# Row maxima of the larger query tiles: turned by a small product and placed by a 4 KB DMA, where the queries were transposed a second time

## The chip, the cores and the metric

The kernel runs on one core of a Trainium2 chip. The core has a matrix engine (TensorE, PE, with a separate path PEld for loading weights), a vector engine (VectorE, DVE), an activation engine (ScalarE, ACT), a general engine (GpSimd, POOL) and a sync engine (SyncE, SP), from whose queue nearly all transfers are issued. Each engine works through its own instructions in order; semaphores tie the engines together. On-chip memory is SBUF; matrix products land in PSUM, of which the kernel holds eight banks. The metric is the device time of one execution in microseconds.

## The reference

A macaron block over an input of 2 x 1024 tokens of width 1024: half a feed-forward layer, attention, half a feed-forward layer, each behind a layer norm and added to the residual. Cut to what matters:

```python
x = x + 0.5 * ffn(layernorm(x))      # gate, top 2 of 8, base weights, LoRA of rank 16 each
x = x + attention(layernorm(x))
x = x + 0.5 * ffn(layernorm(x))

# attention: 32 query heads, 8 key/value heads of 32 columns, causal
q, k = rope(h @ Wq), rope(h @ Wk)
att = q k^T / sqrt(32), masked above the diagonal
out = softmax(att) @ (h @ Wv) @ Wo
```

The softmax needs the maximum of each row of scores before the exponentials are taken. How this maximum comes to the place where it is subtracted is what the change is about.

## The kernel before, in words

The 2048 tokens are cut into 16 query tiles `t` of 128 tokens, eight to a batch element. Query tile `t` looks at `L = t % 8 + 1` key tiles (causal). Numbers are held as pairs of 16-bit halves, so that a product in 16 bits is as exact as one in 32 bits.

**Queries.** `q_out` (L556) writes the queries of a tile into `qst[t % 2]`, 128 tokens by 32 heads by 128 columns. Columns 0 to 95 of a head hold the query in three copies (high, high, low half), columns from 96 on are zero. `qt_load` (L626) takes the eight heads of two key/value heads (a pair `g - 1`, `g`) and transposes them through a DMA from SP's queue into a tile `qt` of 128 rows by 8 heads by 128 tokens, 256 KB. The keys, in `kts`, have three copies in rows 0 to 95 as well, rows 96 to 111 hold the constant -32768, the rest zero.

**First pass, `unit_s1` (L635).** For each key tile, four products `q^T k` give scores with the tokens in the partitions (L650, PE), into one of the three PSUM buffers `p_s1`, and VectorE reduces them to row maxima (L667). On the diagonal key tile, where `L > 2`, ScalarE copies the scores (L661), GpSimd masks them (L662) and VectorE reduces the copy. After the second head of a pair, L676 takes the maximum over the key tiles.

**The maximum into the queries.** The maximum, divided by 32768, is written as a high and a low half. Two ways exist:

- `L <= MPE` (3): the halves go into `mm`, 128 tokens by 16 columns at its end (L681, L682). `turned` remembers the pair. `turn_maxima` (L693) is called after the first score tile of the next unit, or by `unit_s2` if that comes first. It multiplies `mm` by an identity (L697), which turns the halves into rows 96 to 111 of a `p_s1` buffer, and VectorE spreads them over the eight heads in rows 96 to 111 of the `qt` tile that the first pass used (L699).
- `L > 3`: VectorE writes the halves into columns 96 and 97 of the eight heads in `qst` (L687, L688), and `qt_load` transposes these heads a second time into a new `qt` tile (L689).

Ten query tiles (`t % 8` from 3 to 7, twice) of four pairs each take the second way: 40 of the 104 transpositions issued at L630.

**Second pass, `unit_s2` (L799).** For each key tile one product `k^T q` over all 128 rows (L809, into `p_s2`) gives the scores with the keys in the partitions, and rows 96 on subtract the maximum. ScalarE takes the exponential (L815), which `av_batch` multiplies with the values (L745) and, after pairwise sums (`pair`, L723, DVE), with ones.

**Order.** `step(s)` runs one query tile: for each head the key tiles of `unit_s2`, with a piece of the first pass (`look`, `LOOK` = 6 to 3 heads ahead) and pieces of the dense layers (`stage_a1`, `stage_a2`, `stage_c1`, `stage_c2`; products at L409 to L411) between them. Streamed weights come through three buffers of 1 MB, `ws`, from SP's queue (L421). The normed rows are transposed by DMA (`tt`, L338) as are the keys (L553). A scheduler in the compiler layer then orders each engine's instructions by priority, by what waits for what, and by modelled durations. The `qt` pool has five buffers, `mm` is a single buffer.

Of the kernel before, what the change touches and what calls it, by code (L numbers as in the profile page):

```python
# [10 lines left out]
HP = mybir.dt.float16  # L11
I32 = mybir.dt.int32
AF = mybir.ActivationFunctionType
ALU = mybir.AluOpType
# [3 lines left out]
NH, NKV, DH, GRP = 32, 8, 32, 4  # L18
E, R = 8, 16
P = 128  # L20
KB = D // P
NT = B * T // P
TPB = T // P
EPS = 1e-5
XS = 1024.0
MROW = 32768.0
# [9 lines left out]
MPE = 3  # L36
# [8 lines left out]
def kernel(  # L45
# [16 lines left out]
    nc = tc.nc  # L62
# [5 lines left out]
    small = ctx.enter_context(tc.tile_pool(name="small", bufs=SB))  # L68
# [22 lines left out]
        out=cmask, in_=cmask, compare_op=ALU.is_ge, fill=-NEG, base=0,  # L91
# [6 lines left out]
        out=tri, in_=tri, compare_op=ALU.is_gt, fill=0.0, base=0,  # L98
# [9 lines left out]
    MR = 3 * DH  # L108
    MC = 2 * 2 * GRP
    ident16 = const.tile([P, P], HP)  # L110
# [3 lines left out]
    for i in range(2):  # L114
        nc.gpsimd.affine_select(
            out=picks, in_=picks, compare_op=ALU.not_equal, fill=1.0, base=-(MR + 2 * GRP * i),
# [12 lines left out]
    mms = stat.tile([P, MR + MC], HP, name="mm")  # L129
    nc.gpsimd.memset(mms, 0.0)  # L130

    xts, Ts = {}, {}
# [405 lines left out]
    KT, VA, QS, CTX, CT = {}, {}, {}, {}, {}  # L538
# [87 lines left out]
    def qt_load(t, g):  # L626

        assert ready[t] == 2 or g * GRP < NH // 2
        q = qtp.tile([P, 2 * GRP, P], HP, name="qt")
        nc.sync.dma_start_transpose(  # L630
            out=q, in_=QS[t][:, g * GRP : (g + 2) * GRP, :].rearrange("p h c -> p (h c)")
        )
        return q

    def unit_s1(t, g):  # L635

        b0 = t - t % TPB
        L = t - b0 + 1
        odd = g % 2
        if not odd:  # L640
            Ts["mx"] = small.tile([P, 2, TPB, GRP], FP, name="mx", bufs=2)
        mx = Ts["mx"]
        q = Ts["q1", (t, g - odd)][:, odd * GRP : (odd + 1) * GRP, :]
        for j in reversed(range(L)):
            ps = p_s1.tile([P, GRP, P], FP, name="s1")
            diag = j == L - 1
            off = diag and L > LOFF
            pem = diag and not off
            for h in range(GRP):
                nc.tensor.matmul(  # L650
                    ps[:, h, :], lhsT=q[0 : 3 * DH, h, :], rhs=KT[b0 + j][0 : 3 * DH, g, :],
                    start=(not pem or h == 0), stop=not pem,
                )
            if pem:
                nc.tensor.matmul(
                    ps, lhsT=negid, rhs=cmask.unsqueeze(1).to_broadcast([P, GRP, P]),
                    start=False, stop=True,
                )
            if off:
                sm = pp.tile([P, GRP, P], FP, name="sm", bufs=1)  # L660
                nc.scalar.copy(sm, ps)  # L661
                nc.gpsimd.affine_select(  # L662
                    out=sm, in_=sm, compare_op=ALU.is_ge, fill=-3.0e38, base=0,
                    pattern=[[0, GRP], [-1, P]], channel_multiplier=1,
                )
                ps = sm
            nc.vector.tensor_reduce(mx[:, odd, j, :], ps, AX.X, ALU.max)  # L667
            if turned:
                turn_maxima()
            yield  # L670
        if not odd:
            return
        q1 = Ts.pop(("q1", (t, g - 1)))
        if L > 1:
            m = small.tile([P, 2, GRP], FP, name="m4")
            nc.vector.tensor_reduce(m, mx[:, :, 0:L, :].rearrange("p a j h -> p a h j"), AX.X, ALU.max)  # L676
        else:
            m = mx[:, :, 0, :]
        if L <= MPE:
            mm = mms[:, MR:].rearrange("p (i a h) -> p i a h", i=2, a=2)  # L680
            nc.vector.tensor_scalar(mm[:, 0], m, 1.0 / MROW, None, ALU.mult)  # L681
            nc.vector.scalar_tensor_tensor(mm[:, 1], m, 1.0 / MROW, mm[:, 0], ALU.mult, ALU.subtract)  # L682
            turned.append((t, g - 1, q1))
            return
        qs = QS[t][:, (g - 1) * GRP : (g + 1) * GRP].rearrange("p (a h) c -> p a h c", a=2)
        mh, ml = qs[:, :, :, 3 * DH], qs[:, :, :, 3 * DH + 1]
        nc.vector.tensor_scalar(mh, m, 1.0 / MROW, None, ALU.mult)  # L687
        nc.vector.scalar_tensor_tensor(ml, m, 1.0 / MROW, mh, ALU.mult, ALU.subtract)  # L688
        Ts["q2", t, g - 1] = qt_load(t, g - 1)  # L689

    turned = deque()

    def turn_maxima():  # L693

        t, g, q1 = turned.popleft()
        ps = p_s1.tile([P, GRP, P], FP, name="s1")[:, 0, :]
        nc.tensor.matmul(ps[0 : MR + MC], lhsT=mms, rhs=ident16, start=True, stop=True)  # L697
        rows, heads = slice(MR, MR + MC), [MC, 2 * GRP, P]
        nc.vector.tensor_tensor(  # L699
            q1[rows], ps[rows].unsqueeze(1).to_broadcast(heads),  # L700
            picks[rows].unsqueeze(2).to_broadcast(heads), ALU.mult,
        )
        Ts["q2", t, g] = q1
# [95 lines left out]
    def unit_s2(t, g):  # L799
        b0 = t - t % TPB  # L800
        L = t - b0 + 1
        odd = g % 2
        while ("q2", t, g - odd) not in Ts:
            turn_maxima()
        q = (Ts.pop if odd else Ts.get)(("q2", t, g - odd))[:, odd * GRP : (odd + 1) * GRP, :]
        cs = S["cs", g // 4]
        for j in range(L):
            ps = p_s2.tile([P, GRP, P], FP, name="s2")
            ins = nc.tensor.matmul(  # L809
                ps.rearrange("p h k -> p (h k)"), lhsT=KT[b0 + j][:, g, :],  # L810
                rhs=q.rearrange("p h k -> p (h k)"), start=True, stop=True,
            )
            s2_ins.append(ins.ins)
            p32 = pp.tile([P, GRP, P], FP, name="p32", bufs=8)
            nc.scalar.activation(p32, ps, AF.Exp, scale=cs)  # L815
            if j == L - 1:
                nc.gpsimd.affine_select(  # L817
                    out=p32, in_=p32, compare_op=ALU.is_ge, fill=0.0, base=0,
                    pattern=[[0, GRP], [1, P]], channel_multiplier=-1,
                )  # L820
            av_add(t, g, j, L, p32)
            yield
# [46 lines left out]
    for h in range(2):  # L869
        for src, c in ((a_in, slice(0, P)), (g_in, slice(P, P + E))):  # L870
            pin(
                nc.sync.dma_start(
                    out=agst[:, h, :, c],
                    in_=src[h * (D // 2) : (h + 1) * (D // 2), :].rearrange("(k p) n -> p k n", p=P),
# [137 lines left out]
    def look(u):  # L1012

        while maxima[0] < min(u, len(units)):
            v = maxima[0]
            maxima[0] += 1
            if v % 2 == 0 and v + 2 < limit[0]:
                qt1(v + 2)
            yield from unit_s1(*units[v])
# [139 lines left out]
```

## Time and profile before

| | |
|---|---|
| three runs | 1466.78, 1469.46, 1469.99 us (median 1469.46) |
| the profiled execution | 1466.47 us, of which the profile's span is 1464.6 us |
| granted TensorE clock, mean | 0.989 |
| ACT busy | 720.2 us (49%) |
| POOL busy | 369.3 us (25%) |
| DMA queue of SP | 237.25 MB in 248,624 packets, 58.0% of 16 engines' span |
| packets under 512 bytes | 217,072 of 254,863 |

The span is what the profiler saw from the first to the last instruction; what lies between it and the device time (1.87 us) is start and end. A busy share is an average over the whole span: the kernel has stretches of dense products and stretches of attention, and tiles with many key tiles differ from those with few. Matmul ends in the trace are modelled, and matmuls overlap, so the busy share of PE overstates the work.

### The profile page before, as it was taken

The numbers are of one execution on the slowest core, as the hardware profiler recorded it, in microseconds if no ns is written. First come the engines' busy times: TensorE is split into PE (matmuls) and PEld (weight loads), VectorE is DVE, ScalarE is ACT, GpSimd is POOL, SyncE is SP. The second block draws the span as 40 slices with busy tenths as digits, with TensorE's granted clock in tenths as the row PEclk, the third lists the DMA queues.
The fourth block names the chain that finished last, engine by engine and source line by source line (L and its number), as shares of the span: only waits on it lengthen the run. The fifth ranks groups of instructions, "written<-read, shape, count | busy, mean of one in ns | idle before, by whom it ended". The sixth has DMA issues, their size and how long they took to land.

```text
span 1464.6 us, 35179 instructions
## 1 busy us (share of the span) xinstructions
PE 1392.4 (95%) x14636; PEld 786.9 (54%) x14636; DVE 1084.9 (74%) x2416; ACT 720.2 (49%) x1233; POOL 369.3 (25%) x578
## 2 busy tenths in 40 slices
PE   5897999999999999999999899999999999999998
PEld 3443445555556555556554455555555555556544
DVE  6878768968678687787754686868778688789743
ACT  7574434535456455464541343545545455555521
POOL 3352223323222131221211232322222122221220
PEclk9998999999999999999999999999999999999999
DMA  8958397585875837935649759697794855933552
GB/s 303 278 178 197 105 258 200 118 275 147 235 205 102 277 92 180 256 75 166 199 122 290 187 151 262 158 258 185 177 270 66 258 132 106 276 75 88 131 160 85
DMA packets 254863, 266.75 MB, mean 182 GB/s; under 512 B 217072, under 2 KB 220144, under 8 KB 234992
## 3 DMA queue, kind: packets, MB, share of 16 engines
q1 hardware_dynamic: 248624, 237.25, 58.0%
q0 software_dynamic: 4640, 16.78, 6.5%
q10 hardware_dynamic: 1440, 10.49, 2.0%
q8 instruction: 114, 1.87, 0.5%
q14 instruction: 45, 0.37, 0.1%
HBM read 191.60 MB, written 20.45 MB: 145 GB/s over the span
## 4 chain that ended last, share of the span: by engine, by line
PE 76%; DVE 11%; DMA 7%; issue 1%; ACT 1%; POOL 0%; SPq 0%; DVEq 0%; ACTq 0%; POOLq 0%
PE pd L409 15%; PE pd L410 15%; PE pd L411 14%; PE av L745 12%; PE s L809 7%; PE s L650 7%; DVE mx L667 4%; DMA qt<-qst 3%; DMA ws<-wstr 2%; DMA tt<-hl 2%; DVE pair L723 2%; DVE bst L379 1%; DVE xt L496 1%; PE pd L492 1%; PE pd L592 1%
## 5 line engine op out<-in xcount | busy, mean ns | idle before, releaser
L815 ACT ACTIVATE p<-s,cs 128x512 f32<-128x512 f32 x576 | 381.3, 687 | 299.7 <-PE s L809 297.1
L667 DVE TENSOR_REDUCE mx<-s 128x4 f32<-128x512 f32 x480 | 316.0, 677 | 43.2 <-PE s L650 39.1
L723 DVE TENSOR_TENSOR pair<-p,p 128x512 f32<-128x512 f32 x256 | 180.5, 708 | 69.1 <-ACT p L815 36.0
L650 PE MATMUL s<-kts,qt 96*128 96x128 f16 x2304 | 217.2, 221 | 6.1 <-DVE mx L667 3.1
L809 PE MATMUL s<-qt,kts 128*128 128x512 f16 x576 | 211.3, 384 | 10.5 <-DMA qt<-qst 7.0
L650 PEld LDWEIGHTS <-qt 96*128 96x128 f16 x2304 | 164.7, 98 | 97.4 <-issue 28.2
L409 PE MATMUL pd<-ws,tt 128*128 128x512 f16 x544 | 207.1, 381 | 9.2 <-DMA ws<-wstr 7.0
L410 PE MATMUL pd<-ws,tt 128*128 128x512 f16 x544 | 206.7, 380 | 0.0
L411 PE MATMUL pd<-ws,tt 128*128 128x512 f16 x544 | 206.6, 380 | 0.0
L409 PE MATMUL pd<-wb,tt 128*128 128x512 f16 x512 | 196.0, 383 | 2.4 <-DVE xt L496 1.5
L409 PEld LDWEIGHTS <-tt 128*128 128x128 f16 x1312 | 129.1, 98 | 127.3 <-DMA tt<-hl 12.6
L410 PE MATMUL pd<-wb,tt 128*128 128x512 f16 x512 | 195.6, 382 | 1.1 <-DVE wb L217 1.1
L411 PE MATMUL pd<-wb,tt 128*128 128x512 f16 x512 | 195.7, 382 | 0.0
L411 PEld LDWEIGHTS <-tt 128*128 128x128 f16 x1312 | 129.0, 98 | 121.8 <-issue 5.5
L410 PEld LDWEIGHTS <-tt 128*128 128x128 f16 x1312 | 129.2, 98 | 120.7 <-issue 15.2
L817 POOL TENSOR_SCALAR_AFFINE_SELECT p<-p 128x512 f32<-128x512 f32 x128 | 91.5, 717 | 347.2 <-ACT p L815 347.1
L745 PE MATMUL av<-p,va 128*32 128x128 f32 x4608 | 166.6, 278 | 1.4 <-POOL p L817 1.4
L745 PEld LDWEIGHTS av<-p,va 128*32 128x32 f32 x4608 | 115.7, 110 | 59.5 <-issue 42.4
L662 POOL TENSOR_SCALAR_AFFINE_SELECT sm<-sm 128x512 f32<-128x512 f32 x96 | 67.4, 702 | 159.6 <-ACT sm L661 154.0
L745 PE MATMUL av<-pair,ones 128*32 128x128 f32 x2048 | 86.8, 276 | 1.3 <-DVE pair L723 1.2
L661 ACT COPY sm<-s 128x512 f32<-128x512 f32 x96 | 56.0, 583 | 62.0 <-PE s L650 59.2
L527 POOL TENSOR_TENSOR t<-qs,sinT 128x256 f32<-128x256 f32 (+1 forms) x48 | 35.7, 745 | 185.9 <-ACT qs L518 184.8
(205 smaller groups left out, 1821.9 us busy)
## 6 DMA issues: line engine op xcount, KB each, us to landing
ws<-wstr SPq DMA_DIRECT2D x142, 1024.0 KB, 5.7
xt<-hb POOLq DMA_DIRECT2D x32, 512.0 KB, 6.3
wstr<-ws ACTq DMA_DIRECT2D x10, 1024.0 KB, 6.5
xt<-in_x_dram SPq DMA_DIRECT2D x16, 512.0 KB, 3.9
out_dram<-xt SPq DMA_DIRECT2D x15, 512.0 KB, 2.8
st<-in_wo_dram SPq DMA_DIRECT2D x3, 1024.0 KB, 10.9
ws<-in_wb_dram SPq DMA_DIRECT2D x2, 1024.0 KB, 8.3
qst<-in_wb_dram SPq DMA_DIRECT2D x2, 1024.0 KB, 12.6
```

What stands on the lines that cost most here:

```text
L409: nc.tensor.matmul(ps, lhsT=th, rhs=wh, start=(k == 0), stop=False)
L410: nc.tensor.matmul(ps, lhsT=th, rhs=wl, start=False, stop=False)
L411: nc.tensor.matmul(ps, lhsT=tl, rhs=wh, start=False, stop=(last and k == KB - 1))
L650: nc.tensor.matmul(ps[:, h, :], lhsT=q[0 : 3 * DH, h, :], rhs=KT[b0 + j][0 : 3 * DH, g, :], start=(not pem or h == 0), stop=not pem,)
L661: nc.scalar.copy(sm, ps)
L662: nc.gpsimd.affine_select(out=sm, in_=sm, compare_op=ALU.is_ge, fill=-3.0e38, base=0, pattern=[[0, GRP], [-1, P]], channel_multiplier=1,)
L667: nc.vector.tensor_reduce(mx[:, odd, j, :], ps, AX.X, ALU.max)
L723: nc.vector.tensor_tensor(sums, us[i][1], us[i + 1][1], ALU.add)
L745: prev = nc.tensor.matmul(av[rows, i, :], lhsT=w, rhs=p32[:, h, :], start=(us[0][0] == 0 and n == 0), stop=(last and n == len(runs) - 1), ...
L809: ins = nc.tensor.matmul(ps.rearrange("p h k -> p (h k)"), lhsT=KT[b0 + j][:, g, :], rhs=q.rearrange("p h k -> p (h k)"), start=True, stop ...
L815: nc.scalar.activation(p32, ps, AF.Exp, scale=cs)
L817: nc.gpsimd.affine_select(out=p32, in_=p32, compare_op=ALU.is_ge, fill=0.0, base=0, pattern=[[0, GRP], [1, P]], channel_multiplier=-1,)
```

## The change

All tiles write the two halves of the maximum into `mm` and are remembered in `turned`. `turn_maxima` now tells the tiles apart. For tiles with four and more key tiles (`t % 8 >= 3`) only the 16 columns of the maxima are multiplied by the identity, to 16 rows in the partitions 0 to 15 of a `p_s1` buffer; VectorE copies them as 16-bit numbers into `tm` (a single buffer); and a DMA from SP's queue moves these 16 rows of 128 into rows 96 and 97 of the first pass's `qt` tile, eight heads in each, 4 KB in all. The second pass then uses this tile. Tiles with fewer key tiles are handled as before.

```diff
@@ unit_s1 @@
-        if L <= MPE:
-            mm = mms[:, MR:].rearrange("p (i a h) -> p i a h", i=2, a=2)
-            nc.vector.tensor_scalar(mm[:, 0], m, 1.0 / MROW, None, ALU.mult)
-            nc.vector.scalar_tensor_tensor(mm[:, 1], m, 1.0 / MROW, mm[:, 0], ALU.mult, ALU.subtract)
-            turned.append((t, g - 1, q1))
-            return
-        qs = QS[t][:, (g - 1) * GRP : (g + 1) * GRP].rearrange("p (a h) c -> p a h c", a=2)
-        mh, ml = qs[:, :, :, 3 * DH], qs[:, :, :, 3 * DH + 1]
-        nc.vector.tensor_scalar(mh, m, 1.0 / MROW, None, ALU.mult)
-        nc.vector.scalar_tensor_tensor(ml, m, 1.0 / MROW, mh, ALU.mult, ALU.subtract)
-        Ts["q2", t, g - 1] = qt_load(t, g - 1)
+        mm = mms[:, MR:].rearrange("p (i a h) -> p i a h", i=2, a=2)
+        nc.vector.tensor_scalar(mm[:, 0], m, 1.0 / MROW, None, ALU.mult)
+        nc.vector.scalar_tensor_tensor(mm[:, 1], m, 1.0 / MROW, mm[:, 0], ALU.mult, ALU.subtract)
+        turned.append((t, g - 1, q1))
@@ turn_maxima @@
         t, g, q1 = turned.popleft()
         ps = p_s1.tile([P, GRP, P], FP, name="s1")[:, 0, :]
+        if t % TPB >= MPE:
+            nc.tensor.matmul(ps[0:MC], lhsT=mms[:, MR:], rhs=ident16, start=True, stop=True)
+            tm = small.tile([P, P], HP, name="tm", bufs=1)
+            nc.vector.tensor_copy(tm[0:MC], ps[0:MC])
+            nc.sync.dma_start(out=q1[MR : MR + 2], in_=tm[0:MC].unsqueeze(1))
+            Ts["q2", t, g] = q1
+            return
         nc.tensor.matmul(ps[0 : MR + MC], lhsT=mms, rhs=ident16, start=True, stop=True)
```

## The prediction

> **What bounds the kernel now.** I read the busy shares first, then the chain of work that ended last, then the waits of the stretches in which the changed tiles run, then single instructions in time.
>
> ```profile
> PE 1392.4 (95%) x14636; PEld 786.9 (54%) x14636; DVE 1084.9 (74%) x2416; ACT 720.2 (49%) x1233; POOL 369.3 (25%) x578
> ...
> PE 76%; DVE 11%; DMA 7%; issue 1%; ACT 1%; POOL 0%; SPq 0%; DVEq 0%; ACTq 0%; POOLq 0%
> PE pd L409 15%; PE pd L410 15%; PE pd L411 14%; PE av L745 12%; PE s L809 7%; PE s L650 7%; DVE mx L667 4%; DMA qt<-qst 3%; DMA ws<-wstr 2%; DMA tt<-hl 2%; DVE pair L723 2%; DVE bst L379 1%; DVE xt L496 1%; PE pd L492 1%; PE pd L592 1%
> ```
>
> PE leads, DVE is second, and the transpositions `qt<-qst` stand in the chain with 3%. But 95% is not 95% of PE's speed:
>
> ```profile
> 390.74 0.38 PE L410 MATMUL pd<-ws,tt 128*128 128x512 f16 x1
> 390.96 0.38 PE L411 MATMUL pd<-ws,tt 128*128 128x512 f16 x1
> ...
> 941.10 0.39 PE L650 MATMUL s<-kts,qt 96*128 96x128 f16 x4
> ```
>
> Columns: start, duration (us). 512-wide products follow each other every 0.215 us though each is shown 0.38 long; the four 128-wide ones, at 0.22 each, follow every (0.39 - 0.22) / 3 = 0.056. With such intervals (0.025 for L745, from 48 in 1.45 us) all PE instructions add up to 1204 us, 82% of the span. The rest is standing, mostly too short to show. Waits for transfers in the two stretches of the changed tiles, 262 to 760 and 950 to 1400 us:
>
> ```profile
> PE s L809 <- DMA qt<-qst: 3.6, 4, 1.5
> PEld L650 <- DMA qt<-qst: 1.0, 1, 1.0
> PE s L650 <- DMA qt<-qst: 0.5, 1, 0.5
> PEld L809 <- DMA qt<-qst: 0.5, 1, 0.5
> PEld L409 <- DMA tt<-hl: 0.3, 1, 0.3
> ```
> ```profile
> PE s L809 <- DMA qt<-qst: 3.4, 4, 1.6
> PEld L809 <- DMA qt<-qst: 2.4, 2, 1.8
> PEld L409 <- DMA tt<-hl: 2.0, 1, 2.0
> PE pd L409 <- DMA tt<-hl: 1.6, 1, 1.6
> PEld L650 <- DMA qt<-qst: 1.2, 2, 0.9
> PE s L650 <- DMA qt<-qst: 0.4, 1, 0.4
> PEld L409 <- DMA ws<-wstr: 0.4, 2, 0.2
> PE pd L409 <- DMA ws<-wstr: 0.3, 1, 0.3
> ```
>
> Columns: total us, times, longest. Waits at L809 are for the second transposition: 3.6 + 0.5 + 3.4 + 2.4 = 9.9 us. All others together make 7.7. One of the former in time:
>
> ```profile
> 541.36 0.19 DVE L687 TENSOR_SCALAR qst<-m 128x8 f16<-128x8 f32 x1
> ...
> 544.31 0.18 DVE L688 SCALAR_TENSOR_TENSOR qst<-m,qst 128x8 f16<-128x8 f32 x1
> ...
> 544.52 2.61 SPq L630 DMA_TRANSPOSE qt<-qst  x2
> ...
> 547.81 0.59 PE L809 MATMUL s<-qt,kts 128*128 128x512 f16 x2 [0.84 <-DMA qt<-qst]
> ```
>
> Between L687 and L688 lie 3 us of other DVE work without a gap: the time from a maximum to its use is made by DVE's queue and the transfer, not by PE.
>
> **The change, part by part.**
>
> *Second transpositions gone.* 40 of 104. What the removal can give is bounded by the 9.9 us at L809 and, through emptier DMA engines and SP's queue (40 issues of 1.283 us, the median at L630, go; 40 of 0.319, as at L421, come), by the other 7.7. Most of the latter are single late transfers, so I take half, -3.9 us (bounds 0 and -7.7).
>
> *The turning product.* PE gets 40 more. L697, its sister, shows 245 ns, but in a run of products 128 columns cost 0.056: 40 x 0.056 = +2.3 us (bounds 2.3 and 9.8). It takes one of three `p_s1` buffers until it is copied; I cost that at nothing, because its copy (0.28) holds the buffer shorter than a score tile's reduction (0.68) and the other two buffers cover it; without that cover it is 40 x 0.28 = 11 us.
>
> *DVE.* A copy of 16x128 out of PSUM; nearest row is L489, 128x128, 282 ns. L681 and L682 on `m` (282 and 232) for L687 and L688 (237 and 222) add 55: 40 x 0.337 = 13.5 us of DVE. On the path lies DVE's share of the chain, 11%: +1.5 (bounds 0 and 13.5).
>
> *The new chain.* Before: maximum, L688, SP, transposition (median 4.4 us to landing), L809. After: maximum, L682's successor, product on PE, copy on DVE, SP, 4 KB transfer, L809. PE, DVE and SP each wait in order. Behind PE's wait stand score and dense products; behind DVE's, the reductions that free `p_s1`; behind SP's, weights (L421) and `tt` (L338). The built order of the changed kernel places the product 0.9 to 11.6 us of PE work behind the last score tile of its pair, 5.1 in the median, and DVE needs 0.68 + 0.21 + 0.28 + 0.23 = 1.4 (L667, L676, L681, L682). That work of PE covers the wait for the halves, which I cost at nothing; where DVE is late the cover is gone (sister L697 stood 8.9 us in three of 24 cases).
>
> What decides is how soon L809 comes after the product. Counted with the intervals above, PE work between them is, for the 40 pairs: 0.95 (twice), 1.57, 1.58, 1.68, 1.90, 1.98 (four times), 2.04, 2.68, 3.50 (three times), and 25 times 4.16 or more. The path to be covered: product 0.22 + one DVE reduction in the way 0.68 (L667) + copy 0.28 + transfer.
>
> ```profile
> out_dram<-xt SPq DMA_DIRECT2D x15, 512.0 KB, 2.8
> ...
> qt<-qst SPq DMA_TRANSPOSE x104, 4.4
> ...
> out_dram<-xt SPq DMA_DIRECT2D x2, 256.0 KB, 2.0
> ...
> hb<-hs POOLq DMA_DIRECT2D x1, 4.0 KB, 5.1
> ```
>
> No row shows such a transfer. From 2.8 us for 512 KB and 2.0 for 256, the line meets zero bytes at 1.2; the other end is 5.1, the 4 KB at the start. I take 2.5, between the smallest plain transfer (2.0) and the fastest transposition (3.0). The path is then 3.7 us, and the 15 short pairs fall short by 15 x 3.7 - 31.8 = 23.7 us. That takes the place of 9.9: +13.8. While PE stands, DVE works off reductions that PE would wait for later; all is lost where PE binds, none where DVE does. I take half: +6.9 (bounds with the transfer's two ends: -3.9 and +28).
>
> The Trainium skill speaks against the exchange: DMA: Bandwidth & Descriptors, section Rules for kernel authors, says that a transfer under 64 KB pays mostly overhead, so that a 64th of the bytes does not take a 64th of the time. Its section on anatomy gives a fixed 2.0 us for transfers issued from GpSimd; with 2.0 in place of 2.5 the estimate would be a path of 3.2, a shortfall of 17.1 and 3.3 us less in the sum. Its section on the semaphore's 16 has the transfer run on as many engines as divide both outer sizes, here 2 of 16. No row of this trace shows any of it at this size.
>
> *Sum:* -3.9 + 2.3 + 1.5 + 6.9 = +6.8 us. The profiled execution took 1466.47 us (span 1464.6 and 1.87 around it), 3.0 below the median of the runs, 1469.46. Carried to the median: 1476 us.
>
> **Rivals.**
>
> *Even.* DVE catches up so fully that the new standing costs no more than the old: -3.9 + 2.3 + 1.5 = -0.1, 1469. For it: the 3 us of gapless DVE work above. Against: DVE in the chain has only 11%.
>
> *Faster.* The second load's waits go and little comes instead, because a 4 KB transfer lands in 1.2 us and DVE is free: path 0.22 + 0.28 + 1.2 + 0.3 for hand-overs = 2.0, shortfall of ten pairs 3.5 us, so -6.4 in full, with the rest -6.5: 1463. For it: the line through 2.0 and 2.8. Against: 74% busy DVE. By the half rule the sum turns from slower to even at a path of 2.7 us, and to more than 0.2% faster below 2.1.
>
> *Much slower.* On SP's queue and the DMA engines the small transfer stands behind transpositions and 1 MB of weights (5.7 us to landing) and lands after 3.8 us: path 5.0, shortfall 15 x 5.0 - 31.8 + 2.4 = 45.6, half of the excess +17.9: 1487. For it: L338 holds SP for a median of 3.6 us and stands just before the small transfer in 10 of 40 places of SP's built order, L421 in 13. Against: L630 lands within 3.2 us in the lines above.
>
> That the change doesn't do what it says I exclude: the built order has 64 loads of `qt` and 40 small transfers.
>
> **How the numbers follow.** Forecast 0.48 (1472.5 to 1484), even 0.20, faster 0.22, much slower 0.10. About 0.2%, 2.9 us, is what a measurement of this kernel can tell from no change. So slower 0.58, same 0.20, faster 0.22. The range 1463 to 1490 leaves out the far half of the faster case and the far part of the slowest one.
>
> **What would show it.** `qt<-tm` 40 times at 2.5 us to landing (1.2 or 3.8 speak for the outer rivals); PE at L809 waiting for it some 24 us over about 15 pairs, above all the heads where L809 follows the product within 2 us; product and copy at 0.22 and 0.28 or less; waits for `tt` and `ws` in the two stretches halved. I am wrong if waits at L809 stay under 10 us, or if they reach 20 us and the span doesn't grow.

## The result, and the profile after

The changed kernel takes 1483.38 us (median of 5 runs, 1480.84 to 1484.09). The kernel before, on the same chip, takes 1467.74 us (5 runs, 1463.96 to 1469.99). The ratio is 1.0107, with a 95% interval of 1.0086 to 1.0129: slower by 15.6 us. The profiled execution took 1484.09 us, its span is 1482.3 us.

The page of the changed kernel, first its busy times, then its chain of work that ended last:

```profile
PE 1403.6 (95%) x14676; PEld 789.6 (53%) x14676; DVE 1091.5 (74%) x2456; ACT 723.4 (49%) x1233; POOL 366.8 (25%) x578
...
PE 69%; DVE 13%; DMA 6%; issue 3%; ACT 3%; POOL 2%; SPq 1%; ACTq 0%; POOLq 0%; DVEq 0%
PE pd L409 13%; PE pd L410 13%; PE pd L411 13%; PE av L745 10%; PE s L809 7%; PE s L650 6%; DVE mx L667 4%; DMA tt<-hl 3%; DVE pair L723 2%; DMA ws<-wstr 2%; ACT p L815 1%; DVE bst L379 1%; DMA qt<-tm 1%; DVE xt L496 1%; DVE hl L335 1%
```

PE and DVE have 40 instructions more, as the change says. No engine's share has moved by more than a point. PE's part of the chain fell from 76% to 69%: what is new in the chain is not one large wait but more of DVE, ACT, POOL and "issue". The transpositions `qt<-qst`, 3% before, are out of the fifteen lines shown; the small transfer `qt<-tm` has 1%.

The new operations, asked for by the tile `tm` (columns: count, then ns shortest, median, longest; below, us and times):

```profile
L693 DVE CAST tm<-s x40: 236/278/280, 282.2 to 1379.0; 16x128 f16<-16x128 f32 x40
L694 SPq DMA_DIRECT2D qt<-tm x40: 611/643/807, 282.5 to 1379.3; - x40
its engine sat idle before it (us, times) until:
  PE s L691: 19.6, 16
who waited for it (us, times):
  POOL sm L662: 13.1, 2
  PE s L809: 3.4, 7
  PE s L650: 0.8, 2
```

PE waits at L809 for the small transfer for 3.4 us in all. That is less than the 9.9 us that it waited there for the second transpositions. DVE stands 19.6 us ahead of the copy, until the product is done. PE's waits for transfers in the two stretches of the changed tiles, 262 to 775 us, then 960 to 1420 us (total us, times, longest):

```profile
PEld L409 <- DMA tt<-hl: 3.8, 2, 2.4
PE pd L409 <- DMA tt<-hl: 2.9, 2, 1.9
...
PE s L809 <- DMA qt<-tm: 1.0, 3, 0.6
```
```profile
PEld L409 <- DMA tt<-hl: 2.9, 1, 2.9
...
PE pd L409 <- DMA tt<-hl: 2.7, 1, 2.7
PE s L809 <- DMA qt<-tm: 2.4, 4, 0.9
PE pd L409 <- DMA ws<-wstr: 0.4, 1, 0.4
```

The waits for `tt` went from 0.3 and 2.0 + 1.6 us to 3.8 + 2.9 and 2.9 + 2.7. All waits of this kind together are 16 us, where they were 17.6. So the 15.6 us do not stand in the list of waits.

They come bit by bit. Taking the start of the first L809 of a query tile in both traces, the changed kernel is 1.6 us ahead at tile 4, and behind by 6.0 at tile 7, 10.7 at tile 11, 8.1 at tile 12, 16.5 at tile 14 and 20.7 at the last tile run, 8. Measured by issue intervals as in the prediction, PE has 2 us more of work (the 40 products at 0.056 each) and some 15 more of standing.

One of the new products in time:

```profile
1268.88 0.39 PE L650 MATMUL s<-kts,qt 96*128 96x128 f16 x4
...
1269.19 0.22 PE L691 MATMUL s<-ident,mm 128*16 128x128 f16 x1
1269.35 0.10 PEld L809 LDWEIGHTS <-kts 128*128 128x128 f16 x1
1269.35 0.39 PE L809 MATMUL s<-qt,kts 128*128 128x512 f16 x1
...
1269.45 0.28 DVE L693 CAST tm<-s 16x128 f16<-16x128 f32 x1 [1.49 <-PE s L691]
...
1269.76 0.65 SPq L694 DMA_DIRECT2D qt<-tm  x1
```

Four products of 0.056 each end their intervals at 1268.88 + 0.22 = 1269.10; the product starts 0.09 later, and the next one 0.16 after that. This 0.25 is typical where a score or dense product stands ahead: over the 40 products I count 5.3 us ahead of them (37 times 0.08 to 0.13, the rest 0.96, 0.73 and 0.32) and 6.2 us behind them. The copy waited 1.49 us for PE, and the transfer is issued 0.3 us after it.

### The profile page after: what moved, and what is told of

It is laid out like the page before. It is cut to its first block, busy times and chain, and to the rows that moved or that the text cites. A ratio compares the mean times of both kernels' runs of the same rounds, so it can differ in the third digit from the quotient of the medians.

```text
span 1482.3 us, 35310 instructions
## 1 busy us (share of the span) xinstructions
PE 1403.6 (95%) x14676; PEld 789.6 (53%) x14676; DVE 1091.5 (74%) x2456; ACT 723.4 (49%) x1233; POOL 366.8 (25%) x578
## 4 chain that ended last, share of the span: by engine, by line
PE 69%; DVE 13%; DMA 6%; issue 3%; ACT 3%; POOL 2%; SPq 1%; ACTq 0%; POOLq 0%; DVEq 0%
PE pd L409 13%; PE pd L410 13%; PE pd L411 13%; PE av L745 10%; PE s L809 7%; PE s L650 6%; DVE mx L667 4%; DMA tt<-hl 3%; DVE pair L723 2%; DMA ws<-wstr 2%; ACT p L815 1%; DVE bst L379 1%; DMA qt<-tm 1%; DVE xt L496 1%; DVE hl L335 1%
## 5 line engine op out<-in xcount | busy, mean ns | idle before, releaser
L650 PE MATMUL s<-kts,qt 96*128 96x128 f16 x2304 | 213.6, 220 | 7.5 <-DVE mx L667 3.7
L809 PE MATMUL s<-qt,kts 128*128 128x512 f16 x576 | 208.0, 383 | 9.7 <-ACT p L815 6.0
L409 PE MATMUL pd<-ws,tt 128*128 128x512 f16 x544 | 207.5, 381 | 10.1 <-DMA ws<-wstr 5.5
L650 PEld LDWEIGHTS <-qt 96*128 96x128 f16 x2304 | 160.9, 98 | 94.2 <-issue 32.1
L817 POOL TENSOR_SCALAR_AFFINE_SELECT p<-p 128x512 f32<-128x512 f32 x128 | 87.3, 684 | 337.0 <-ACT p L815 336.8
L745 PE MATMUL av<-p,va 128*32 128x128 f32 x4608 | 165.6, 277 | 1.8 <-POOL p L817 1.8
L745 PEld LDWEIGHTS av<-p,va 128*32 128x32 f32 x4608 | 115.1, 109 | 60.1 <-issue 41.9
L662 POOL TENSOR_SCALAR_AFFINE_SELECT sm<-sm 128x512 f32<-128x512 f32 x96 | 66.8, 696 | 236.1 <-ACT sm L661 195.2
L745 PE MATMUL av<-pair,ones 128*32 128x128 f32 x2048 | 86.5, 275 | 2.1 <-DVE pair L723 2.1
L768 POOL TENSOR_TENSOR tt<-pair,tt 128x256 f16<-128x256 f32 x64 | 50.1, 784 | 118.9 <-ACT tt L767 118.7
```

The costliest lines, as they stand in the source:

```text
L409: nc.tensor.matmul(ps, lhsT=th, rhs=wh, start=(k == 0), stop=False)
L650: nc.tensor.matmul(ps[:, h, :], lhsT=q[0 : 3 * DH, h, :], rhs=KT[b0 + j][0 : 3 * DH, g, :], start=(not pem or h == 0), stop=not pem,)
L662: nc.gpsimd.affine_select(out=sm, in_=sm, compare_op=ALU.is_ge, fill=-3.0e38, base=0, pattern=[[0, GRP], [-1, P]], channel_multiplier=1,)
L745: prev = nc.tensor.matmul(av[rows, i, :], lhsT=w, rhs=p32[:, h, :], start=(us[0][0] == 0 and n == 0), stop=(last and n == len(runs) - 1), ...
L809: ins = nc.tensor.matmul(ps.rearrange("p h k -> p (h k)"), lhsT=KT[b0 + j][:, g, :], rhs=q.rearrange("p h k -> p (h k)"), start=True, stop ...
L817: nc.gpsimd.affine_select(out=p32, in_=p32, compare_op=ALU.is_ge, fill=0.0, base=0, pattern=[[0, GRP], [1, P]], channel_multiplier=-1,)
```

## The experiments

**The stand-in.** All experiments use a stand-in for the kernels: each DMA transposition is replaced by a plain transfer of as many bytes, in pieces of 256 bytes that are read 112 numbers apart, on the same queue at the same place in the program, and the exponential's scale is set to 0 so that all numbers stay finite. It thus leaves out the turning of rows, queries and keys, and so the result of the dense layers and of attention. It can't show what is special to a transposition: PE's waits at the second pass for the second load are 0.3 us in it, where they were 7.0 (3.6 + 3.4) in the kernel before. Line numbers are shifted by one to four; the second pass's L809 is L808 in the stand-in of the changed kernel. Below, every time without a range is the median of a stand-in. The runs were made in three groups; the unchanged kernel before ran in each, with 1470.62, 1470.35 and 1470.58 us, so that the groups can be laid beside each other. Ratios are to this kernel; 0.001 is 1.5 us.

Three theories stood at the start, and a fourth, array mode, came after the first group of runs. *Late transfer*: the maxima reach the second pass late, as the prediction has it. *Blocked VectorE*: the copy stands at the head of VectorE's queue until PE has made the product, and holds up what is behind it. *Order*: the planner's other order costs by itself, whatever is in it. *Array mode*: with the 16-column product PE runs empty before and after it, so that it takes far longer than its 0.056 us.

**Does the stand-in show the change at all?** Stand-ins of the kernel before and of the changed kernel:

> Stand-in for the kernel before, the base of all that follows: each of the 160 DMA transpositions is replaced by a plain transfer of as many bytes from the same place to the same place in pieces of 256 bytes, so rows aren't turned; the scale of the exponential is zero, so that all numbers stay finite. Every other instruction stays. All theories: within 2% of 1467.7 us, with the second transfer of the queries still 40 times in place.

> The changed kernel with the same stand-in for its 120 transpositions. If the loss of 15.6 us lies in the product, the copy, the small transfer and the order, it should come again: 10 to 20 us above the stand-in for the kernel before. If it lies in the transpositions themselves (their weight on the queues), it should be gone: within 4 us or below.

Measured 1454.29 us (ratio 0.9897, 0.9859 to 0.9936) and 1470.98 us (1.0012, 0.9994 to 1.0029): +16.7 us, where the kernels themselves differ by 15.6. The loss does not hang on anything special to the transposition, and the stand-in is fit for taking the change apart. That the steps below have the same sizes in the kernels themselves is not shown.

**The floor: neither way for the larger tiles.** The halves, the product, the copy, the transfer and the second load are left out for tiles with four and more key tiles, so their maxima are not subtracted:

```diff
+        if L > MPE:
+            Ts["q2", t, g - 1] = q1
+            return
```

> Stand-in, and for tiles with four and more key tiles nothing carries the maximum into the queries: no halves, no product, no copy, no transfer, no second load; the second pass uses the first pass's queries. The floor. Late-transfer theory (PE waits at L809 for the new transfer): 8 to 15 us below the stand-in for the kernel before. Blocked-VectorE theory (the copy waits in VectorE's queue for a product that stands late in PE's queue: 16 waits, 19.6 us in the trace of the changed kernel, and 40 x 0.28 us of copies): the same. Order theory (the scheduler's other order costs by itself, whatever is in it): not below the stand-in for the kernel before.

Measured 1446.49 us (0.9848, 0.9818 to 0.9879), 7.8 under the stand-in of before. This is the price of the second load with the two instructions that write its halves. It is just short of the 8 to 15 that two of the theories expected; the order theory expected no gain, and falls in this plain form.

**Only the halves and the product.** The product's rows are then not used:

```diff
             nc.tensor.matmul(ps[0:MC], lhsT=mms[:, MR:], rhs=ident16, start=True, stop=True)
-            tm = small.tile([P, P], HP, name="tm", bufs=1)
-            nc.vector.tensor_copy(tm[0:MC], ps[0:MC])
-            nc.sync.dma_start(out=q1[MR : MR + 2], in_=tm[0:MC].unsqueeze(1))
```

> Stand-in; in tiles with four and more key tiles halves and 16-column product are made, but not copied and not moved; the second pass subtracts nothing there and waits for nothing. Array-mode theory: 9 to 13 us above the floor without any of it (1446.5), 1455 to 1460, most of what separates the changed kernel from the floor beside the copy. Late-transfer theory: 2 to 6 above the floor.

Measured 1452.23 us (0.9884, 0.9864 to 0.9904): +5.7. That is less than array mode asks for.

**Product and copy, no transfer.** Only the `dma_start` is left out, so the maxima stay in `tm`:

> Stand-in; product and copy on VectorE, but no transfer; the second pass waits for nothing of it and subtracts nothing. The step to the stand-in for the changed kernel (1471) is then the transfer and the wait for it. Late-transfer theory: that step is 8 us or more. Array-mode theory with a small price for the copy: 1459 to 1466 here, the step 3 to 8.

Measured 1457.95 us (0.9919, 0.9896 to 0.9943): another +5.7. The transfer with all that hangs on it is then worth 1470.98 - 1457.95 = 13.0 us, the largest step, as the late transfer theory says.

**The copy on ScalarE.**

```diff
-            nc.vector.tensor_copy(tm[0:MC], ps[0:MC])
+            nc.scalar.copy(tm[0:MC], ps[0:MC])
```

> Stand-in for the changed kernel with the copy to tm on ScalarE (49% busy) in place of VectorE (74%); everything else stays. Blocked-VectorE theory: 8 to 16 us below the stand-in for the changed kernel. Late-transfer theory: within 4 us of it. Order theory: no forecast.

Measured 1469.2 us (1.0002, 0.9981 to 1.0023): -1.8, inside the intervals. DVE's idle time ahead of the copy (17.7 us in the stand-in) costs nothing that can be seen here. Blocked VectorE falls as the main cause.

**The product with all 112 columns**, in the form of its sister L697 (rows 96 to 111 are then copied and moved), and the same with the copy on ScalarE:

```diff
-            nc.tensor.matmul(ps[0:MC], lhsT=mms[:, MR:], rhs=ident16, start=True, stop=True)
+            nc.tensor.matmul(ps[0 : MR + MC], lhsT=mms, rhs=ident16, start=True, stop=True)
```

> Stand-in for the changed kernel with the product made as in tiles with few key tiles: all 112 columns of mm as weights, rows 96 to 111 of the result copied and moved. Same bytes, same number of instructions on every engine. Array-mode theory (16 columns of weights put TensorE into its 128x32 mode, and it runs empty before and after: in the trace of the changed kernel the 40 products take 5.3 us ahead of them and 6.2 behind, 0.29 each, where the 112-column ones take nothing ahead and 0.06 behind): 40 x 0.2 = 8 us below the stand-in for the changed kernel (1471), 1460 to 1465. Late-transfer theory and order theory: within 3 us of it.

> Stand-in for the changed kernel, product with all 112 columns and copy on ScalarE. If array mode and VectorE's blocked queue are two separate prices: 2 to 6 us below the one with the wide product alone. If VectorE's queue costs nothing: within 2 us of it. Beats the stand-in for the kernel before (1454.3) only if nothing of the transfer's wait remains, which I don't expect: 1457 to 1463.

Measured 1475.23 us (1.0042, 1.0028 to 1.0057) and 1470.26 us (1.001, 0.9995 to 1.0025). The time that PE gives to the 40 products did fall, from 5.2 + 6.1 us ahead and behind to 5.3 + 3.2, but the kernel did not get faster: 4.2 us above the stand-in of the changed kernel, with intervals that just touch. Both runs miss the range that was expected of them. Array mode is a true price on PE of some 3 us, and not the cause. The copy on ScalarE gains 5.0 us beside the wide product (intervals apart), where it gained 1.8 beside the narrow one. This is what the expectation gives for a separate price of VectorE's queue, so a price of a few us for it is not excluded in that form.

**Is it the transfer, or the waiting for it?** The transfer stays, from the same rows on the same queue, but goes to spare rows that nothing reads, so the second pass runs without maxima and need not wait:

```diff
-            nc.sync.dma_start(out=q1[MR : MR + 2], in_=tm[0:MC].unsqueeze(1))
+            nc.sync.dma_start(out=tm[MC : 2 * MC], in_=tm[0:MC])
```

> Stand-in of the changed kernel in which the small transfer is made as before, from the same tile, of the same 16 pieces of 256 bytes, on the same queue, but into a spare place that nothing reads; the second pass takes the queries' rows as they are, so it no longer waits for maxima. Compare with 1471.0 us (stand-in of the changed kernel) and 1458.0 (its product and copy without the transfer). If the +13.0 between those two comes from the transfer itself (its issue on SyncE's queue, what stands behind it there, its packets), this stays at 1468 to 1473. If it comes from the second pass having to wait for the maxima, this falls to 1455 to 1461.

Measured 1456.84 us (0.9908, 0.9889 to 0.9927), 14.1 us under the stand-in of the changed kernel and level with the run that has no transfer at all (1457.95). The tile `tm` in this run:

```profile
L693 SPq DMA_DIRECT2D tm<-tm x40: 557/580/7548, 283.0 to 1358.6; - x40
...
DMA to landing us min/median/max: 1.7/2.2/10.1
```

Forty transfers are issued at 0.58 us each, land after 2.2 us in the median, and cost nothing that can be seen when nobody waits for them. SP's queue and the DMA engines are cleared. So is GpSimd's wait for the copy, 13.1 us ahead of L662 in the changed kernel: it is 25.6 us in this run. In the trace of the changed kernel SP's queue tells the same: from the last write of `hl` to the issue of its `tt` transposition I count 7.8 us over all 40, against 20.3 before.

**The dependence without a transfer.** The copy goes straight into rows 96 and 97 of the queries, as 2 rows of 128 numbers that are not the whole maxima:

```diff
-            tm = small.tile([P, P], HP, name="tm", bufs=1)
-            nc.vector.tensor_copy(tm[0:MC], ps[0:MC])
-            nc.sync.dma_start(out=q1[MR : MR + 2], in_=tm[0:MC].unsqueeze(1))
+            nc.vector.tensor_copy(q1[MR : MR + 2, :, 0:16], ps[0:2].rearrange("p (a b) -> p a b", b=16))
```

> Stand-in of the changed kernel in which there is no small transfer: the copy of the product goes from PSUM straight into the two rows of the transposed queries, 2 rows of 128 numbers (they are not the whole maxima), so that the second pass depends on VectorE's copy and not on a DMA. If the +13.0 comes from the transfer itself or from the 1.8 to 3.7 us that it puts between copy and second pass, this gives 1455 to 1461. If the dependence alone costs it, however short the way, 1466 to 1473.

Measured 1462.86 us (0.9942, 0.9921 to 0.9963), between the two expectations. Waiting for the copy costs 6.0 us (its interval just touches that of the run above), and the way through the transfer another 8.1 (intervals apart).

**More distance.** One line, for the changed kernel and for the kernel before:

```diff
-LOOK = [6, 6, 4, 4, 3, 3, 3, 3]
+LOOK = [6, 6, 4, 4, 4, 4, 4, 4]
```

> Stand-in of the changed kernel with the first pass one unit further ahead of the second on tiles 4 to 7 of each batch (look-ahead 4 in place of 3, nothing else). If the maxima come too late for the second pass, a unit more of distance takes most of the +13.0 back: 1458 to 1465. If the cost isn't lateness but work and order (product, copy, transfer), it stays at 1468 to 1475.

> The same look-ahead of 4 in the stand-in of the kernel before (1454.3 with 3). Needed to read the run above: if a unit more of distance is worth something by itself, both fall by as much. Lateness theory: this one changes by under 3 us (1451 to 1458), since the second load has its distance already, or gets slower, since the sums and buffers of the first pass are held longer; work-and-order theory: both change by the same amount within 3 us.

Measured 1463.12 us (0.9949, 0.9929 to 0.9969) and 1463.76 us (0.9958, 0.9941 to 0.9976). A unit more of distance takes 7.9 us from the one and puts 9.5 on the other, and with it the change costs -0.6 us in place of +16.7. Those who wait for `tm` in the stand-in of the changed kernel, first with the old distance, then with the new:

```profile
  POOL sm L661: 13.1, 2
  PE s L808: 1.4, 3
  PE s L649: 0.3, 1
```
```profile
  PE s L649: 1.1, 3
```

With the new distance the second pass (L808 here) doesn't appear any more. Why the larger distance costs the kernel before 9.5 us wasn't tried; its trace shows PE's waits for weights, `ws<-wstr`, at 6.3 us where the smaller distance has 4.2, and those of the first pass for its queries, `qt<-qst`, at 3.4 where it has 0.5. Together that is about half of it. Nor does the longer distance help beyond the old design: neither of the two is under 1454.29.

**Where the waiting is, if not at L808.** Worked out from the traces of the stand-ins by issue intervals: PE's standing time ahead of some kinds of products (of all kinds in the first row), and its work between a pair's last score tile and its first L808, as a mean over the 40 pairs. `p_deaf` is the run with the transfer that nobody reads, `p_direct` the one without a transfer, `p_after` the stand-in of the changed kernel, `p_slack` the same with more distance.

```
us                         p_deaf  p_direct  p_after  p_slack
standing, all               282.3     283.0    296.0    287.2
  ahead of L808              20.8      22.0     28.2     23.7
  ahead of pd<-ag,tt         11.7      11.7     15.6     11.1
  ahead of pd<-wb,tt         14.3       9.8     14.8     11.7
work to first L808            9.0       9.7     11.6     16.6
```

The first row holds some 110 us in every column that are no standing: the products of L745 start in fours, 6, 6, 7 and 88 ns apart, and the count gives each at most 25 ns. The differences between columns stay. The standing grows with the way through the transfer, by 13.0 us from `p_direct` to `p_after`. From the stand-in of the kernel before to `p_after` such a count gives 17 us, spread over many places: 5 ahead of the new product, 4 ahead of the first pass (L649), 4 ahead of `pd<-ag,tt`, 3 ahead of L808, and 3 less ahead of `pd<-ws,tt`. Only 2.0 us of the 28.2 ahead of L808 are ahead of the first L808 of a pair of the larger tiles, the one that needs the new rows; 19.7 are ahead of later ones. And the second pass stands further back in PE's order than in `p_deaf` and `p_direct`: the compiler layer, which orders by modelled durations, has put other work ahead of it. So the lateness is not waited out at the instruction that needs the row; that it is built into the order is likely, but not shown. That place is not the price: in the floor run it is 12.3 us of work, and that is the fastest of all, and in the stand-in of the kernel before it is some 13. Nor do the waits for `tt` decide, which rose with the change: in the floor run they are 13.3 us (weights) and 10.2 (products), in `p_after` 13.5 and 10.9, at 24.5 us between the two times. Through which places the order turns into standing stays open.

## Why the prediction was right in sign and half in size

The forecast was +6.8 us, made to 1476 us; it is +15.6, and 1483.38 us lies inside its range. Its terms stand below beside the ladder of the stand-ins, which adds up to +16.7. The prediction sets the 9.9 us of waits that go against the 23.7 that come, and then halves. To lay it beside the steps, half of 9.9 is added here to the -3.9 of the second load, and the new wait stands with half of 23.7:

```
                                     forecast   measured
second load (with its halves) gone       -8.9       -7.8
product (measured with the halves)       +2.3       +5.7
copy (halves forecast here)              +1.5       +5.7
transfer itself                             0       -1.1
second pass waits for the copy          +11.9       +6.0
... and for the transfer                            +8.1
```

The single steps carry an uncertainty of some 3 to 5 us, since each is a difference of two ratios known to about 0.002 to 0.003; the sum and the last step are firmer. Of the 9.9 us that the forecast lacks, 7.6 lie in the product and the copy.

- *Removal.* Right in sign and near in size. But the view it was read from doesn't explain it: the waits at L809 are nearly absent in the stand-in (0.3 us), and the second load costs 7.8 us there all the same.
- *Product.* The step "in a run of products 128 columns cost 0.056" failed. The product isn't in a run; ahead of it and behind it PE loses 11.5 us over 40, above even the upper bound of 9.8. Some of that would be standing anyway, and the run with it alone shows 5.7, halves included.
- *DVE.* The forecast took 11% of 13.5 us, DVE's share of the chain; the copy alone costs 5.7. The share of a chain in the kernel before is no measure of what a step on a new chain costs.
- *New chain, the transfer.* Well sized: 2.5 us was assumed, 2.2 is the median in `p_deaf`, and the shortest time from issue to an L809 that had waited is 1.8 in the changed kernel. The way ahead of it was taken too long: from the product's start to the issue it is 0.70 in the median of the changed kernel, where the prediction adds up 1.18. With a path of 0.70 + 2.2 = 2.9 in place of 3.7, its own sum gives +1.7, which is inside the 2.9 us that it takes for no change. (It puts the turn from slower to even at a path of 2.7; by its sum and the 2.9 us it is 3.1.) So the right sign owes something to luck.
- *New chain, the place.* Here the mechanism failed: "PE at L809 waiting for it some 24 us over about 15 pairs". It is 3.4 us, 7 times, and by the prediction's own words it is wrong there. The mechanism behind it, that the second pass comes too soon after its maximum, is what the runs show: 14.1 us hang on this dependence and none on the transfer. The wrong part was to look for it in one wait. Half of the shortfall, 11.9, is close to the 14.1 of the dependence; since it was counted for a wait that didn't come, and with a path too long, this is luck and no confirmation.
- *Waits for `tt` and `ws` halved.* Wrong: those for `tt` rose. SP's emptier queue did shorten the way from `hl` to the issue of `tt`, and no gain from it shows.
- *PE's work.* With the intervals that the prediction gives, PE's instructions add up to 1282 us, 88% of the span, not 1204 and 82%: the 1204 comes out when the fours of L745 are counted short, as above. No term of the sum rests on it.

The rivals: *even* and *faster* fell with the measured time. *Much slower* named 1487 us, nearer to the measured time than the forecast is, but its mechanism fell: the small transfer does not stand behind SP's queue, lands after 2.2 us in the median (10.1 at most), and costs nothing that shows where nobody waits for it. *Array mode*, *blocked VectorE* and *order*, thought of after the result, fell as main causes.

## What to carry to other kernels

A step that is put between a value and its use can cost by the distance that is left there, not by its own duration: here 40 transfers of 4 KB were free without a reader, and the reader's dependence on copy and transfer cost 14 us, half of it to be had back by one more unit of distance (which by itself made the kernel before slower). In a kernel whose order a planner builds, such a lateness can show as standing spread over other products; a short list of waits at the reader is no proof that it was in time. The test is to cut the dependence and leave the work.

## What the hardware showed that was not expected

- What a product with 16 columns of weights costs depends on its neighbours. Behind a product with 128 columns (23 of the 40 in the changed kernel) it starts 0.09 us later than the interval asks for, and the next product starts 0.16 after it; the form with 112 columns has 0 and 0.06 there (22 of 40, `p_wide`, the run with all 112 columns). That is 0.19 more for the narrow one. Behind an L745, whose weights have 32 columns (17 of the 40), it starts 0.09 after the last of them, and the next product 0.15 after it; the form with 112 columns has 0.20 and 0.10 there (18 of 40), which is 0.06 more than the narrow one. A score or dense product directly behind an L745 also starts 0.2 after it, and an L745 behind such a product 0.09 late. So PE loses time at each change between narrow and wide weights. The Trainium skill, TensorEngine Tiling (Array Packing), section Key Properties, says that a change of the tiling mode drains the engine; the trace agrees in kind, if these are such changes, which it doesn't tell. The profile's durations show nothing of this: 219 to 223 ns for 16 columns, 242 in the median for 112 in `p_wide`.
- A transfer of 4 KB between two places of SBUF lands 1.7 us after its issue at the least, 2.2 in the median (`p_deaf`), where 256 KB to the chip's main memory took 2.0: a 64th of the bytes does not make it faster.
